# Quantizing in place, loading x earlier, and handing out averages and band runs one portion per score tile: a two-layer macaron kernel on one core

## The chip, the core and the metric

The kernel runs on one core of a Trainium2 chip. The metric is the device time of one execution in microseconds (us). A core has five engines that matter here: PE (TensorE, matmuls, with its weight loads shown apart as PEld), DVE (VectorE), ACT (ScalarE), POOL (GpSimd), and SP (SyncE), whose queue issues nearly all DMAs. Each engine works through its own instructions in order; semaphores join them.

## The reference, cut to what matters

Sixteen sequences of 512 tokens with 128 features pass through two layers. Layer 0, which the change touches, is a half-step feed-forward network, an attention, and the same feed-forward network again:

```
x = x + 0.5 * ffn(layernorm(x))      # both inputs of each matmul quantized to FP4 in blocks of 16
x = x + attn(layernorm(x))           # 16 heads of 8 features
x = x + 0.5 * ffn(layernorm(x))

# attn: relative positions clipped to +-64
dist  = clip(idx[None,:] - idx[:,None], -R, R) + R
score = einsum('bhqd,bhkd->bhqk', q, k) + einsum('bhqd,qkd->bhqk', q, rel_emb_k[dist])
attn  = softmax(score)
ctx   = einsum('bhqk,bhkd->bhqd', attn, v) + einsum('bhqk,qkd->bhqd', attn, rel_emb_v[dist])

# fp4 quantize and dequantize, blocks of 16
scale = max(max|xb| / 6, 1e-12);  q = GRID[searchsorted(MID, |xb/scale|)] * sign(xb) * scale
```

Layer 1 (mixture of experts with a small attention inside, linear attention, mixture of experts) follows; its code is the same in both kernels.

## The kernel before, in words

**Units.** Layer 0 works on halves of sequences. A unit `u = 2*b + half` holds the 256 query tokens of half `half` of sequence `b`; there are 32 units. For a unit, the scores of all 16 heads against 512 keys are cut into 4 key tiles `kt` of 128 keys and 8 blocks `bb` of 32 queries: 32 score tiles of 128 x 512, one PSUM bank each.

**Two passes over the scores.** `maxima` computes each score tile once (L263, and L267 for the relative positions where the tile is near the diagonal, "in the band") and reduces it on DVE with L341 (`mx`). At the end of a unit the maxima go through a small chain (`mk`, `mt`, `mn`) and two rounds of DMA (`MD`, then row 28 of `BD`), so that the second pass gets scores with the maximum already subtracted. `main` computes the tiles again and ACT takes the exponential into `PT` (L369), a buffer per key tile with three slots. Score tiles of both passes share a PSUM pool with three banks (`pS`, tiles `sps`). The maxima run about one and a half units ahead of the exponentials (47 tiles).

**Averages and band runs.** After the 8 score tiles of a key tile, `main` issues 16 matmuls `PT` times `V` that accumulate in `av0` and `av1` (L272, L274: "the averages"). Where all key tiles that reach a group of four query blocks are done, it issues the matmuls with the relative value embeddings into `rps` (same lines: a "band run" for two blocks at a time), and four ACT copies from `rps` to `RV` (L403: "band copies"). In half 0 the two groups are complete after `kt` 1 and 2, in half 1 both after `kt` 3. At the end of a unit, `RV` goes to DRAM (`RD`) and comes back reordered (`cr`), and ACT copies `av` to `cx` (L412). `av0`, `av1` and `rps` have one buffer each.

**Around it.** `fin` of a unit adds `cx` and `cr`, divides (L430 to L434), projects (L437 to L440) and adds into x. `head` and `tail` are the two feed-forward networks, each run on half a tile of x by `half`: layer norm (L55 to L62), the quantizer `quant_steps` (L65 to L82), matmuls (L121, L125), the quantizer again, matmuls (L139). `prep` and `prepV` make q, k and v for a later tile. The quantizer writes its scaled copy into a buffer `q_y` and its rounding constant into `q_M`.

**The order.** Each of these is a Python generator that yields between steps. `interleave` holds them all, each with a number of steps `n` and a stretch from `f` to `t` in units of `u`, and always advances the one whose next step is due first:

```
k=min(live,key=lambda r:r[3]+(r[4]-r[3])*r[2]/r[1])
```

`main` counts 59 steps in its unit: 32 score tiles, four empty steps after each key tile's averages, two after each band run of two blocks, one after the band copies, one at the end. The maxima of all units are one generator with 33 steps a unit. What is issued this way is then ordered on each engine by the framework's scheduler, which also hands out buffers; `run` keeps the matmuls of one burst together.

**x.** A tile of x (the 512 tokens of one sequence, 256 KB) lives in the pool `xk` with five buffers, from its load (`xload`, called in `head`, three of them before the loop) to the store of its tail to `X2` (L486). `head` of tile b+3 starts 0.1 units before unit 2b.

Of the kernel before, what the change touches and what calls it, by code (L numbers as in the profile page):

```python
# [8 lines left out]
F32 = mybir.dt.float32  # L9
# [16 lines left out]
class K:  # L26
# [37 lines left out]
    def quant_steps(s, X, wk, P, nb, tag):  # L64

        nc=s.nc
        n=nb*16
        X3=X.rearrange("p (b k) -> p b k",k=16)
        sc=wk.tile([128,nb],F32,name=tag+"_sc"); ri=wk.tile([128,nb],F32,name=tag+"_ri")
        nc.vector.tensor_reduce(sc[:P],X3,axis=AX.X,op=ALU.max,apply_absolute_value=True)  # L70
        nc.vector.tensor_scalar(sc[:P],sc[:P],float(np.float32(1/6)),1e-12,ALU.mult,ALU.max)
        nc.vector.reciprocal(ri[:P],sc[:P]); yield
        y=wk.tile([128,max(704,n)],F32,name=("q_y","q_yw")[n>704])[:,:n]; y3=y.rearrange("p (b k) -> p b k",k=16)
        nc.vector.tensor_tensor(y3[:P],X3,ri[:P].unsqueeze(2).to_broadcast([P,nb,16]),ALU.mult); yield
        M=wk.tile([128,max(704,n)],F32,name=("q_M","q_Mw")[n>704])[:,:n]
        nc.vector.tensor_scalar(M[:P].bitcast(U32),y[:P].bitcast(U32),0x7F800000,None,ALU.bitwise_and)
        nc.vector.tensor_scalar(M[:P],M[:P],1.0,C_MAG,ALU.max,ALU.mult); yield
        nc.vector.scalar_tensor_tensor(y[:P],y[:P],SHRINK,M[:P],ALU.mult,ALU.add); yield  # L78
        nc.gpsimd.tensor_tensor(M[:P],y[:P],M[:P],ALU.subtract)  # L79
        M3=M.rearrange("p (b k) -> p b k",k=16)  # L80
        nc.gpsimd.tensor_tensor(M3[:P],M3[:P],sc[:P].unsqueeze(2).to_broadcast([P,nb,16]),ALU.mult)
        yield M  # L82

class FFN:
# [22 lines left out]
    def half(f, xb, half, wk, pp):  # L107

        s=f.s; nc=s.nc
        xh=xb[:,2*half:2*half+2,:]  # L110
        xn=wk.tile([128,2,128],F32,name="f_x")
        yield from s.ln_steps(xh,xn,wk,2)
        for xq in s.quant_steps(xn.rearrange("p a b -> p (a b)"),wk,128,16,"xq"): yield
        ps=pp.tile([128,512],F32,name="mps")
        for j in range(2): nc.tensor.transpose(ps[:,j*128:(j+1)*128],xq[:,j*128:(j+1)*128],s.ident)
        xqT=wk.tile([128,256],F32,name="f_x"); nc.scalar.copy(xqT,ps[:,:256]); yield
        h=wk.tile([128,2,I],F32,name="f_h")
        for j in range(2):
            t=h[:,j,:]
# [26 lines left out]
class Attn0:  # L146
# [119 lines left out]
                w0=kt*128-blk*32-x+a.OFF  # L266
                nc.tensor.matmul(out[:,x*64:x*64+64],a.ET[:,w0:w0+128],TQ[:,:,b*32+4*x:b*32+4*x+4],start=False,stop=(x==7),skip_group_check=True)  # L267

    xnT={}; pend={}; last=None
    def run(a, mms):  # L270

        r=a.nc.tensor.matmul(*mms[0][0],**mms[0][1])  # L272
# [85 lines left out]
    def main(a, b, half, X, wk, big, pS, pA, pM):  # L358
        s=a.s; nc=a.nc; i=b%2
        u=(2*b+half)%3; BD=a.BD[u]; TQ=a.TQ[u]; KS=a.KS[b%2]; V=a.V[b%2]; RD=a.RD[half]; cr=a.cr[0]  # L360
        av=[pA.tile([128,512],F32,name=f"av{z}") for z in range(2)]
        RV=wk.tile([128,4,4,4,16],F32,name="RV")
        PT=[None]*4
        for kt in range(4):
            pt=big.tile([128,16,256],F32,name="PT"); PT[kt]=pt
            for bb in range(8):
                ps=pS.tile([128,512],F32,name="sps")
                a.scores(ps,kt,half,bb,BD,TQ,KS)
                nc.scalar.activation(pt[:,:,bb*32:bb*32+32].rearrange("p h (x j) -> p x h j",j=4),ps.rearrange("p (x h j) -> p x h j",x=8,j=4),AF.Exp)  # L369
                yield  # L370
            vs=a.vers(kt,half)
            mms=[]
            for z in range(4):
                for cg in range(4):
                    h=z*4+cg
                    o=av[z//2][cg*32:cg*32+32,(z%2)*256:(z%2)*256+256]
                    fs=(kt==0 and z%2==0)
                    mms.append(((o,V[:,2*kt-1+vs,h*9:h*9+32],pt[:,h,:]),dict(start=fs,stop=(kt==3),skip_group_check=True,tile_position=(0,cg*32))))
            a.run(mms)
            for _ in range(4): yield  # L380
            for hb in range(2):
                bl=range(hb*4,hb*4+4)
                ks=[k for k in range(4) if any(a.inband(k,half*8+x) for x in bl)]
                if max(ks)!=kt: continue
                rps=pA.tile([128,512],F32,name="rps")
                first=[True]*4
                mms=[]
                for b0 in bl[::2]:
                    ok=[(bb,k) for k in reversed(ks) for bb in (b0+1,b0) if a.inband(k,half*8+bb)]
                    for n,(bb,k) in enumerate(ok):  # L390
                        blk=half*8+bb
                        for x in range(8):
                            cg=x%4; col=(bb-hb*4)*128+(x//4)*64
                            v0=(blk*32-k*128+a.UO)//8
                            mms.append(((rps[cg*32:cg*32+32,col:col+64],a.TV[a.vers(k,half)][:,x,v0-8*a.vers(k,half):v0-8*a.vers(k,half)+4,:].rearrange("p v d -> p (v d)"),
                                PT[k][:,:,bb*32+4*x:bb*32+4*x+4]),
                                dict(start=first[cg],stop=(k==min(q for p,q in ok if p==bb)),skip_group_check=True,tile_position=(0,cg*32))))
                            first[cg]=False
                    a.run(mms); mms=[]
                    yield  # L400
                    yield
                for c in range(4):
                    nc.scalar.copy(RV[:,:,c,:,hb*8:hb*8+8].rearrange("p j z a -> p a z j"),rps.rearrange("p (a z c j) -> p c a z j",a=8,z=4,j=4)[:,c])  # L403
                yield

        nc.sync.dma_start(RD[:,:4*8*1024].rearrange("x (r f) -> x r f",f=1024),RV)
        for c in range(4):
            src=bass.AP(tensor=RD.tensor,offset=RD.offset+c*64,ap=[[1024,8],[8*1024+256,16],[1,64]])
            nc.sync.dma_start(cr[c*32:c*32+8].rearrange("p (xj f) -> p xj f",f=64),src)
        cx=wk.tile([128,4,256],F32,name="cx")  # L410
        for zz in range(2):
            nc.scalar.copy(cx[:,2*zz:2*zz+2,:].rearrange("p z (b j x) -> p (z b) x j",j=4,x=8),av[zz].rearrange("p (y x j) -> p y x j",x=8,j=4))  # L412
        a.pend[b,half]=cx,cr
        yield

    def fin(a, b, half, X, wk, pM):

# [28 lines left out]
def interleave(*gens):  # L446

    live=[[g,n,0,f,t] for g,n,f,t in (q if len(q)==4 else (*q,0,1) for q in gens)]
    while live:
        k=min(live,key=lambda r:r[3]+(r[4]-r[3])*r[2]/r[1])  # L450
        try: next(k[0]); k[2]+=1
        except StopIteration: live.remove(k)
# [4 lines left out]
def layer0(tc, s, w, src, dst, nb=16):  # L457
    nc=tc.nc
    tok=lambda x,b: x[b].rearrange("(t p) d -> p t d",p=128)
    P="L0_attn_"; names=["W_qkv","b_qkv","W_out","b_out","rel_emb_k","rel_emb_v"]  # L460
    with ExitStack() as c:
# [5 lines left out]
        pA=c.enter_context(tc.tile_pool(name="pA",bufs=1,space=PS))  # L467
        wk=c.enter_context(tc.tile_pool(name="wk",bufs=1))
        fk=c.enter_context(tc.tile_pool(name="fk",bufs=2))
        xk=c.enter_context(tc.tile_pool(name="xk",bufs=5))  # L470
        X={}
        def xload(b):
            if b in X or b>=nb: return
            t=xk.tile([128,4,128],F32,name="x"); X[b]=t
            nc.sync.dma_start(t,tok(src,b))
        def head(b,h):

            if b<nb: xload(b); yield from F.half(X[b],h,fk,pF)
        def prep(b):
            if b<nb: yield from A.prep(b,X[b],wk,pM)  # L480
        def prepV(b):
            if b<nb: yield from A.prepV(b,pM)
        def tail(b,h):
            if b<0: return
            yield from F.half(X[b],h,fk,pF)
            nc.sync.dma_start(tok(dst,b)[:,2*h:2*h+2,:],X[b][:,2*h:2*h+2,:])  # L486
# [15 lines left out]
                if next(st,0)==0: return  # L502
                yield
        pl,hl=2,3
        W=dict(part=0,V=(.6,.7),fin=(.45,.9),prep=(0,.7),tail=1.0,head=(-.1,1))
        with tc.tile_pool(name="wp",bufs=1) as wp:
            for b in range(3): xload(b)
            F=FFN(s,w["L0_ffn_w_gate"],w["L0_ffn_w_up"],w["L0_ffn_w_down"],wp,pF)
            ffn2=lambda f,b: interleave((f(b,0),21,0,.8),(f(b,1),21,.2,1))
            ffn2(head,0)  # L510
            A=Attn0(s,wp,pS,*[w[P+n] for n in names])
            def run(g):
                for _ in g: pass
            run(prep(0)); run(prepV(0)); loads(0); run(mxs(0,0))
            FFN1.pre(s,wp,[pA.tile([128,512],F32,name=f"av{z}") for z in range(2)]+[pA.tile([128,512],F32,name="rps")],w)
# [3 lines left out]
        for b in range(nb):  # L519
            for h in range(2):  # L520
                u=2*b+h
                def at(g,n,f,t): S.append((g,n,u+f,u+t))
                at(A.main(b,h,X,wk,big,pS,pA,pM),59,0,1)
                fn,tl=(W['fin'],W['tail']) if u<2*nb-2 else ((.3,.5),.6)
                at(A.fin(b,h,X,wk,pM),5,1+fn[0],1+fn[1])
                at(tail(b,h),21,1+fn[1]+.001,1+fn[1]+tl)
                if b+hl<nb: at(head(b+hl,h),21,*W['head'])
                if h==0 and b+pl<nb: at(prep(b+pl),11,*W['prep'])
                if h==1 and b+1<nb: at(prepV(b+1),1,*W['V'])
        interleave(*S)  # L530


# [505 lines left out]
```

## Time and profile before

| | |
|---|---|
| median of the runs | 3629.37 us (3628.54 to 3629.66) |
| the profiled execution | 3633.94 us |
| its span, first to last instruction | 3632.2 us |
| mean granted PE clock | 0.90 |
| busy: PE, DVE, ACT, POOL | 2825.0, 2444.9, 1693.8, 838.9 us |
| exponentials of layer 0 (L369) | 175.5 to 1974.5 us, 1024 of them, 0.60 us each |
| maxima of layer 0 (L341) | 126.4 to 1921.8 us, 1024 of them, 0.70 us each |

How to read it: the first half of the span, to about 2045 us, is layer 0, and 1800 us of that are the 32 units. Busy time of PE is modelled, since matmuls are pipelined. A wait is written as "engine, tile, line <- what ended it: total us, times, longest". In a line of the timeline, the first number is the start in us, the second the time taken, and a bracket at the end gives the idle time of the engine just before and what ended it. PEclk is the granted clock of PE as a share of full speed.

### The profile page before, as it was taken

The page shows a single profiled execution, that of the slowest core. Times are in us where ns is not written, and L with a number is a line of the kernel's source. Part 1 is how long each engine was busy: PE and PEld are TensorE (multiplying, and loading weights), DVE is VectorE, ACT ScalarE, POOL GpSimd, SP SyncE. Part 2 cuts the span into 40 slices and gives each one's busy share as a digit, 9 for nine tenths or more (in the row PEclk, how much of TensorE's full clock was granted, in tenths as well). Part 3 has the DMA queues.
Part 4 walks back from the last instruction along what each step waited for, and adds up shares of the span by engine and source line. Part 5 has one row for each costly group of instructions (what it writes and reads, how often), then busy time and mean ns, then how long its engine had stood idle before and what let it go on. Part 6 is the DMA issues. An engine that isn't in the chain of part 4 may idle for free. (4 is left out here: it accounts for less than half of the span.)

```text
span 3632.2 us, 95259 instructions
## 1 busy us (share of the span) xinstructions
PE 2825.0 (78%) x40077; PEld 2032.3 (56%) x40077; DVE 2444.9 (67%) x6508; ACT 1693.8 (47%) x3391; POOL 838.9 (23%) x789
## 2 busy tenths in 40 slices
PE   5578989889898889888896388873788888878570
PEld 3357777667676677666775244431565555555230
DVE  5568788777887788877773467774546655655356
ACT  3145555545455454545554155533455454445242
POOL 4122222222222222222110222212112211111226
PEclk8799999999999999999998599886899989989785
DMA  3232222321223222222210111104312222121401
GB/s 105 54 91 71 57 53 59 81 63 52 65 65 77 64 50 58 76 74 62 53 33 19 32 33 36 36 33 123 90 54 73 59 63 56 36 62 36 126 17 46
DMA packets 290159, 217.23 MB, mean 60 GB/s; under 512 B 77402, under 2 KB 257476, under 8 KB 289604
## 3 DMA queue, kind: packets, MB, share of 16 engines
q1 hardware_dynamic: 284468, 207.72, 21.6%
q8 instruction: 315, 5.16, 0.6%
q10 hardware_dynamic: 5264, 3.43, 0.4%
q14 instruction: 112, 0.92, 0.1%
HBM read 110.28 MB, written 100.78 MB: 58 GB/s over the span
## 5 line engine op out<-in xcount | busy, mean ns | idle before, releaser
L341 DVE TRANSPOSE_TENSOR_REDUCE mx<-sps 128x16 f32<-128x512 f32 x1024 | 702.5, 701 | 261.7 <-PE sps L263 137.2
L263 PE MATMUL sps<-a_BD,a_KS 128*128 128x128 f16 x8192 | 736.4, 222 | 136.2 <-DVE mx L341 65.6
L369 ACT ACTIVATE PT<-sps 128x512 f32<-128x512 f32 x1024 | 576.4, 599 | 433.8 <-PE sps L267 238.1
L263 PEld LDWEIGHTS <-a_KS 128*128 128x128 f16 x8192 | 546.1, 98 | 296.4 <-issue 260.0
L59 POOL TENSOR_TENSOR ln_rs<-ln_ve,negh 128x4 f32<-128x4 f32 (+1 forms) x192 | 176.9, 930 | 855.1 <-DVE ln_ve L58 760.6
L267 PE MATMUL sps<-a_TQ,a_ET 128*128 128x64 f16 x7168 | 370.3, 195 | 0.0
L721 DVE SCALAR_TENSOR_TENSOR moe<-mps,oh,moe 128x128 f32<-128x128 f32 x896 | 289.8, 341 | 110.7 <-PE mps L719 96.5
L79 POOL TENSOR_TENSOR q_M<-q_y,q_M 128x704 f32<-128x704 f32 (+2 forms) x129 | 157.0, 1218 | 784.6 <-DVE q_y L78 658.6
L719 PE MATMUL mps<-f_W,T 128*128 128x512 f32 x512 | 297.1, 701 | 24.8 <-DVE moe L721 20.0
L267 PEld LDWEIGHTS <-a_ET 128*128 128x128 f16 x7168 | 311.2, 99 | 2.3 <-issue 1.9
L274 PE MATMUL av<-PT,a_V 128*32 128x256 f32 x3840 | 251.9, 387 | 0.0
L894 DVE TENSOR_TENSOR a_at<-pp,a_cm 128x1024 f32<-128x1024 f32 x128 | 154.3, 1214 | 79.6 <-PE pp L892 78.6
L892 PE MATMUL pp<-a_F 64*128 64x128 f32 x2048 | 169.8, 306 | 41.4 <-DVE a_at L894 30.2
L892 PEld LDWEIGHTS pp<-a_F 64*128 64x128 f32 x2048 | 143.3, 206 | 93.0 <-DVE a_at L894 36.9
L719 PEld LDWEIGHTS mps<-f_W,T 128*128 128x128 f32 x512 | 102.7, 222 | 125.0 <-issue 75.3
L274 PEld LDWEIGHTS av<-PT,a_V 128*32 128x32 f32 x3840 | 121.4, 111 | 68.7 <-issue 5.0
L874 ACT ACTIVATE a_F<-pp 128x1024 f32<-128x1024 f32 x128 | 127.0, 1025 | 46.8 <-PE pp L872 40.5
L62 ACT ACTIVATE xn<-xn,ln_mr,ln_rs 128x128 f32<-128x128 f32 x256 | 103.6, 481 | 95.5 <-DVE ln_mr L60 75.2
L274 PE MATMUL rps<-PT,a_TV 128*32 128x64 f32 x6912 | 134.5, 222 | 4.6 <-issue 4.4
L139 PE MATMUL mps<-wdT,hT 128*128 128x128 f32 (+1 forms) x768 | 126.9, 301 | 5.6 <-ACT hT L136 4.0
L673 ACT COPY f_PT<-St 32x512 f32<-32x512 f32 x128 | 78.7, 615 | 106.0 <-DVE St L672 99.9
L872 PE MATMUL pp<-a_QK,a_PK 128*128 128x512 f16 x256 | 82.7, 413 | 54.4 <-DMA a_QK<-a1d 26.6
(342 smaller groups left out, 5330.2 us busy)
## 6 DMA issues: line engine op xcount, KB each, us to landing
QM<-a_HM SPq DMA_DIRECT2D x180, 128.0 KB
a_TQ<-QM SPq DMA_DIRECT2D x120, 192.0 KB
RD<-RV SPq DMA_DIRECT2D x32, 512.0 KB
a_KS<-KSd SPq DMA_DIRECT2D x128, 96.0 KB
a_QK<-a1d SPq DMA_DIRECT2D x128, 96.0 KB
xn<-X SPq DMA_DIRECT2D x32, 256.0 KB
a1d<-a_hi SPq DMA_DIRECT2D x64, 128.0 KB
a_BD<-QS SPq DMA_DIRECT2D x128, 58.0 KB
```

Source lines behind the costliest of these rows:

```text
L59: nc.gpsimd.tensor_tensor(rs,ve,s.negh[:,:n],ALU.pow); yield
L79: nc.gpsimd.tensor_tensor(M[:P],y[:P],M[:P],ALU.subtract)
L263: nc.tensor.matmul(o4[:,g],KS[:,sd,g*512+kt*128:g*512+(kt+1)*128],BD[:,g,:,b*32:b*32+32].rearrange("p h (x j) -> p x h j",j=4),start=(g==0 ...
L267: nc.tensor.matmul(out[:,x*64:x*64+64],a.ET[:,w0:w0+128],TQ[:,:,b*32+4*x:b*32+4*x+4],start=False,stop=(x==7),skip_group_check=True)
L274: for p,q in mms[1:]: a.nc.tensor.matmul(*p,**q)
L341: with a.s.tc.high_priority(): r=nc.vector.tensor_reduce(mx[:,kt,:,bb],ps.rearrange("p (i c) -> p i c",c=32),axis=AX.X,op=ALU.max,apply_tr ...
L369: nc.scalar.activation(pt[:,:,bb*32:bb*32+32].rearrange("p h (x j) -> p x h j",j=4),ps.rearrange("p (x h j) -> p x h j",x=8,j=4),AF.Exp)
L719: nc.tensor.matmul(ps,yT[:,j*128:(j+1)*128],a.W[:,e2*4:e2*4+4,:],start=True,stop=True)
L721: nc.vector.scalar_tensor_tensor(moe[:,j,:],ps[:,e*128:(e+1)*128],oh[:,j,e2*4+e:e2*4+e+1],moe[:,j,:],ALU.mult,ALU.add)
L874: nc.scalar.activation(f,ps,AF.Relu)
L892: nc.tensor.matmul(ps[:,hh,bs],f[hh*64:hh*64+64,1,bs],f[hh*64:hh*64+64,0,bs],start=True,stop=True)
L894: nc.vector.tensor_tensor(k,ps.rearrange("p h (b q) -> p (h b) q",b=4),a.cm.unsqueeze(1).to_broadcast([128,8,128]),ALU.mult)
```

## The change

Four things change in layer 0; no arithmetic and no instruction count does.

1. The quantizer works in place: the scaled copy is written over its input, and `q_y` goes. Tiles named `f_x` get three buffers instead of two.
2. `xk` has seven buffers. Four tiles are loaded before the loop, and tile b+4 is loaded by a generator of its own, due 0.35 units before unit 2b+1, instead of in its head (due 0.1 units before unit 2b+2).
3. Averages, band runs, band copies and the end of a unit become portions in a list `todo`. One portion is taken off after each score tile, so those of a key tile are issued with the score tiles of the next key tile, and those of the last one with the first key tile of the next unit. `main` counts 32 steps. After the last unit, `rest` issues what is left.
4. `fin` is due from 0.6 to 1.0 of the next unit instead of 0.45 to 0.9 (the last two units keep their own times); the tail after it moves with it.

```diff
 # quant_steps
-        y=wk.tile([128,max(704,n)],F32,name=("q_y","q_yw")[n>704])[:,:n]; y3=y.rearrange("p (b k) -> p b k",k=16)
+        y=X; y3=X3
 # FFN.half
-        xn=wk.tile([128,2,128],F32,name="f_x")
+        xn=wk.tile([128,2,128],F32,name="f_x",bufs=3)
...
-        xqT=wk.tile([128,256],F32,name="f_x"); nc.scalar.copy(xqT,ps[:,:256]); yield
+        xqT=wk.tile([128,256],F32,name="f_x",bufs=3); nc.scalar.copy(xqT,ps[:,:256]); yield
 # Attn0
-    xnT={}; pend={}; last=None
+    xnT={}; pend={}; last=None; todo=[]
 # Attn0.main
+        def avrun(kt):
+            if kt==0: T["av"]=[pA.tile([128,512],F32,name=f"av{z}") for z in range(2)]
...
+            a.run(mms)
+        def rvrun(hb, b0, ks):
+            if b0%4==0: T["rps"]=pA.tile([128,512],F32,name="rps"); T["first"]=[True]*4
...
+            a.run(mms)
+        def rvcopy(hb):
+            if hb==0: T["RV"]=wk.tile([128,4,4,4,16],F32,name="RV")
+            for c in range(4):
+                nc.scalar.copy(T["RV"][:,:,c,:,hb*8:hb*8+8].rearrange("p j z a -> p a z j"),T["rps"].rearrange("p (a z c j) -> p c a z j",a=8,z=4,j=4)[:,c])
+        def end():
+            nc.sync.dma_start(RD[:,:4*8*1024].rearrange("x (r f) -> x r f",f=1024),T["RV"])
...
+            a.pend[b,half]=cx,cr
         for kt in range(4):
             pt=big.tile([128,16,256],F32,name="PT"); PT[kt]=pt
             for bb in range(8):
                 ps=pS.tile([128,512],F32,name="sps")
                 a.scores(ps,kt,half,bb,BD,TQ,KS)
                 nc.scalar.activation(pt[:,:,bb*32:bb*32+32]...,AF.Exp)
+                if a.todo: a.todo.pop(0)()
                 yield
-            vs=a.vers(kt,half)
...
-            a.run(mms)
-            for _ in range(4): yield
+            a.todo.append(lambda kt=kt: avrun(kt))
             for hb in range(2):
                 bl=range(hb*4,hb*4+4)
                 ks=[k for k in range(4) if any(a.inband(k,half*8+x) for x in bl)]
                 if max(ks)!=kt: continue
-                rps=pA.tile([128,512],F32,name="rps")
...
-                    a.run(mms); mms=[]
-                    yield
-                    yield
-                for c in range(4):
-                    nc.scalar.copy(RV[...])
-                yield
+                a.todo+=[lambda hb=hb,b0=b0,ks=ks: rvrun(hb,b0,ks) for b0 in bl[::2]]+[lambda hb=hb: rvcopy(hb)]
+            if kt==3: a.todo.append(end)
+    def rest(a):
+        while a.todo: a.todo.pop(0)(); yield
 # layer0
-        xk=c.enter_context(tc.tile_pool(name="xk",bufs=5))
+        xk=c.enter_context(tc.tile_pool(name="xk",bufs=7))
...
-            if b<nb: xload(b); yield from F.half(X[b],h,fk,pF)
+            if b<nb: yield from F.half(X[b],h,fk,pF)
+        def xl(b):
+            xload(b); yield
...
-        W=dict(part=0,V=(.6,.7),fin=(.45,.9),prep=(0,.7),tail=1.0,head=(-.1,1))
+        W=dict(part=0,V=(.6,.7),fin=(.6,1.0),prep=(0,.7),tail=1.0,head=(-.1,1))
...
-            for b in range(3): xload(b)
+            for b in range(4): xload(b)
...
-                at(A.main(b,h,X,wk,big,pS,pA,pM),59,0,1)
+                at(A.main(b,h,X,wk,big,pS,pA,pM),32,0,1)
...
+                if h==1 and b+hl+1<nb: at(xl(b+hl+1),1,-.35,-.3)
...
+        S.append((A.rest(),8,2*nb,2*nb+.15))
         interleave(*S)
```

## The prediction

> **What bounds the kernel now.** I began with the slices of the page, which show no engine full, then took the steady stretch of layer 0 alone, 422 to 1692 us. The first exponentials (L369) of units 4 and 26 start there, so it is 22 units of 57.7 us. The columns are busy time with the instruction count behind it, then clock, DMA share and GB/s.
>
> ```profile
> core 0: us, PE busy (x) PEld busy (x) DVE busy (x) ACT busy (x) POOL busy (x), PEclk, DMA share, GB/s
> 422.00:1692.00 1270.00, 1126.22 (x20068) 889.03 (x20065) 1013.48 (x2274) 647.68 (x1430) 306.91 (x287) 0.98 0.25 64
> ```
>
> Per unit that is 51.2 us of PE, 46.1 of DVE, 29.4 of ACT. PE comes nearest to a bound, but 6.5 us of each unit it stands idle, and the time goes to engines that wait for each other. Who waits for whom in the same stretch (total us, times, longest):
>
> ```profile
> PE sps L263 <- DVE mx L341: 40.1, 45, 3.9
> PE sps L263 <- ACT PT L369: 21.6, 56, 0.8
> PE mps L437 <- DVE a_V L321: 19.2, 11, 1.8
> PE mps L440 <- ACT cn L438: 11.4, 9, 1.8
> DVE ln_st L55 <- DMA x<-in_L_attn_x_dram: 41.1, 10, 5.2
> SPq L475 <- DMA X<-x: 26.0, 10, 3.4
> ```
>
> The first and fifth rows belong together. The head of a new tile of x issues its load when it is due (L475); the fifth buffer is then still being stored, so the load waits on SP, and DVE, which works in order, stands 4.1 us (41.1/10) before the first statistic. Meanwhile the maxima (L341) queued behind it leave the three score buffers full, and PE stops. In time, on DVE and PE:
>
> ```profile
> 879.93 1.07 DVE L55 BATCH_NORM_STATS2 ln_st<-x 128x6 f32<-128x128 f32 x5 [4.11 <-DMA x<-in_L_attn_x_dram]
> 882.54 0.39 PE L263 MATMUL sps<-a_BD,a_KS 128*128 128x128 f16 x4 [2.85 <-DVE mx L341]
> 884.61 0.58 PE L263 MATMUL sps<-a_BD,a_KS 128*128 128x128 f16 x4 [0.42 <-DVE mx L341]
> 884.99 0.63 PE L267 MATMUL sps<-a_TQ,a_ET 128*128 128x64 f16 x8
> 888.38 0.39 PE L263 MATMUL sps<-a_BD,a_KS 128*128 128x128 f16 x4
> ```
>
> The third and fourth rows show a second price: after the stop the same groups take 0.58 and 0.63 us, where they take 0.39 and 0.40 elsewhere, until 888 us.
>
> **The order, before and after.** In the built programs PE's order in units 4 to 25 can be counted. Before, score tiles for the exponentials come 275 times in pairs, 11 times in threes and 121 times alone, and those for the maxima come up to nine in a row. Changed, both kinds alternate: 660 single ones of each and 22 pairs of each. All three engines keep their instructions; layer 1 moves by a few places. A tile costs PE 0.24 us out of the band and 0.47 in it (starts of such groups at 873.18, 873.66 and 873.89 us), ACT 0.60 (L369) and DVE 0.70 (L341).
>
> **The change, part by part.**
>
> *a. x loaded ahead.* The load of tile b+4 stands 1.25 units (72 us) before its head, with seven buffers and no store left to wait for. Thirteen tiles (3 to 15) are loaded inside the loop: 13 x 2.85 us of PE stop = 37 us. Bounds: 0, if DVE's lost time is then lost elsewhere, and 13 x 4.14 = 54. I take 37, since PE is the engine nearest to its bound. What is late next: the same head's scale (L59 on POOL), with a DVE that has work meanwhile.
>
> *b. The slow spells after stops.* A mean clock of 0.98 in the row above is about 0.02 x 1270 = 25 us of lost full clock in 22 units. Bounds 0 and 25; I take 15, as the stops of (a) and (d) that start most of these spells shrink.
>
> The Trainium skill, "TensorE: Matmul & The Clock Gate", section "HAM oscillation — how this bites in real kernels", speaks against (b): its rule is to avoid idle gaps of PE over about 3.4 us, so a stop of 2.85 us should cost nothing more. The rows at 884.61 and 884.99 show that here it did. By the rule (b) is 0 and the forecast 3577 us.
>
> *c. Pairs of exponentials.* PE waits for L369 because two or three such tiles come in a row while ACT needs 0.60 each. With a maxima tile between them this wait has no cause left: 22 us, from the second row. Bounds 0 and 31 (21.6 stretched from 22 units to 32).
>
> *d. The output projection (L437, L440).* Before, L440 stands two tiles behind the transposes whose copy it needs, and PE waits; L437 waits for a DVE that does prepV's V first. With `fin` moved from (.45,.9) to (.6,1) it leaves prepV's place (.6,.7) on DVE, and in the built order four to six tiles and the averages stand between L437 and L440. 19.2 + 11.4 = 31 us at most, 0 at least; I take 20. The last two units keep (.3,.5), so the end of the layer stays.
>
> *e. What the portions add.* The averages of a key tile now stand on PE behind one maxima tile and the first score tile of the next key tile, on average; before, mostly behind two maxima tiles. They need the last exponential, 0.60 us and about 0.1 of hand-over. The two tiles cover 0.47 to 0.94 us. Queued behind a waiting average is everything on PE, and through the three score buffers DVE and ACT. Covered it is 0; never covered 128 x 0.7 = 90 us. The near row is small (L272 waits for L369 in all 7.4 us), so I take 0.1 each, 13 us. In odd units the first band run stands right behind a score tile whose exponential it needs: 16 x 0.7 = 11 us, bounds 0 and 11. The fourth load at the start is 256 KB more at the 146 GB/s of the first 60 us: up to 2 us, and 1 more for reordered starts. Sum +27, bounds 0 and +104.
>
> *f. At nothing.* In place, the quantizer issues the same operations on other buffers. `f_x` and `f_h` are held until POOL's subtraction (L79, 1.67 us at 704 wide); a third `f_x` and the half unit until the next `f_h` cover that. Without cover, one such POOL operation for each of the 64 halves is 107 us at most. Band copies (L403, four of 0.42 us) and `cx` copies (1.08 us) only move to the next key tile; RD's DMAs follow them by up to a quarter unit, 14 us, while `fin` moves 0.15 units, 9 us. On SP these DMAs stand behind the x load and ahead of the QS and QM stores of the tile two ahead, which have over a unit of slack. One X2 store stands among the loads of BD and TQ; if its tail is late, the loads are, with some 28 us until their first score.
>
> Sum: -37 - 15 - 22 - 20 + 27 = -67 us. The profiled execution took 3633.9 (span 3632.2 and 1.7 around it) and the median of the runs is 3629.4, 4.6 lower. So 3567 for a profile like this one and **3562 us** for the median. A unit would fall from 57.7 to about 55.3 us. With all bounds it is 3488 to 3733.
>
> **Rivals.** *Slower: the averages wait.* ACT now has its fixed work in the first key tile of even units, two `cx` copies (2.16 us) and four band copies (1.68) between exponentials. If the last exponential runs late by one such copy, each average stops PE, and everything behind it, by about 1 us: +128 +14 against -94, some 3677 us. It decides from (94-14)/128 = 0.6 us for each average. Against it: ACT is busy 51% of the stretch, and the small row above.
>
> *Hidden anyway.* DVE's 4.1 us may be work that it catches up, as it idles 20% of the time; then only (c) or (d) pays and (e) takes it back: -22 +27 -4 of (d), close to no change, 3630.
>
> *The order matters more than its stops.* If alternation also ends the starving of ACT (L369 waits 154.4 + 113.9 us for PE in the stretch) and the unit falls to PE's present 51.2 us plus 1.5, 32 units gain 5 us each: 3470 us.
>
> *Not what it says.* If the scheduler had put the portions back together there would be no alternation; the built order excludes that.
>
> **How the numbers follow.** Forecast, with its own range 3508 to 3622: 0.62. Slower: 0.19. Hidden: 0.09. More than forecast: 0.10. The range of 3508 to 3650 leaves out most of the last and the upper half of the slower case, under 0.2. About 0.2% (7 us) is what a measurement of this kernel can tell from no change. Faster takes the first, the fourth and a little of the hidden case, 0.74; same 0.07; slower 0.19.
>
> **What would show it.** Right: no L55 wait for x, PE's wait for L341 near 10 us in 22 units, for L369 under 5, clock 0.99, units near 55 us. Wrong: rows "PE av L272 <- ACT PT" of tens of us, L263 still waiting for L341 with DVE full of other work, or L263 waiting for DMA of BD or TQ.

## The result and the profile after

The changed kernel takes 3863.01 us (median of four runs, 3856.82 to 3876.84) against 3629.51 for the kernel before: a ratio of 1.0636, interval 1.0602 to 1.067. It is slower, where the forecast was faster, and lies beyond every bound that the prediction worked out. The profiled execution took 3858.58 us. From its page, the first line and the row of granted clock in 40 slices:

```profile
span 3856.9 us, 95214 instructions
PEclk8788888898889889888999859897699889999775
```

The same row of the kernel before:

```profile
PEclk8799999999999999999998599886899989989785
```

The first half of the clock row, which is layer 0, stands mostly at 8 where the kernel before had 9. The time is lost there: the 32 units run from 181.8 to 2211.6 us, 2029.7 us against 1799.6 before. That is +230.1, and the whole profiled execution grew by 224.6. The same steady stretch as in the prediction, units 4 to 25, in the same columns:

```profile
439.00:1895.00 1456.00, 1168.62 (x20068) 953.69 (x20069) 1056.72 (x2259) 661.30 (x1428) 317.27 (x283) 0.88 0.22 56
```

The 22 units take 186 us more with the same 20068 matmuls: 42 us are PE busy for longer at a clock of 0.88 instead of 0.98 (1168.6 against 1126.2), and 144 us are PE standing still (287.4 against 143.8). The loss is not even. An even unit, in which `prep` runs, takes 74.7 us on average where it took 57.2; an odd one takes 57.7 where it took 58.2. Who waits for whom in this stretch (total us, times, longest):

```profile
DVE qkhi L307 <- DMA QS<-qkhi: 93.9, 11, 9.5
DVE qklo L307 <- DMA KSd<-qklo: 82.6, 11, 7.9
PE sps L263 <- DVE mx L341: 129.7, 31, 8.2
PE sps L349 <- DVE mk L347: 75.7, 22, 4.6
PE mps L434 <- DVE cx L426: 45.6, 22, 3.3
PE sps L263 <- ACT PT L407: 21.3, 61, 0.7
PE rps L272 <- ACT PT L407: 7.7, 11, 0.8
```

The first two rows matter most: DVE, a compute engine, waits for DMAs that *store* what `prep` made. It can't need their data; it needs their buffer. `prep` of an even unit casts q into a buffer of tag `qkhi` and its rest into `qklo` (L143, L144), does the same for k, and stores them to `QS` and `KSd` (L302). Then L307 takes a small product of q apart in the same way, into buffers of the *same tags*. There are two of `qkhi` and one of `qklo`, so L307 has to wait until prep's own stores have landed: (93.9 + 82.6) / 11 = 16.0 us in each even unit. Before, the same line waited for DMAs 5.2 us in all, in the stretch 422 to 1692 us:

```profile
DVE qklo L307 <- DMA KSd<-qklo: 5.2, 5, 1.3
```

L341 is queued behind it on DVE, and PE waits for L341 (third row, 40.1 before). The row for the averages, on which the prediction's slower rival was built, is the last: 0.7 us, 11 times.

Unit 12 in time, on SP's queue, then on DVE, POOL and PE (start, time taken, in brackets the idle time just before and what ended it):

```profile
983.51 0.77 SPq L394 DMA_DIRECT2D RD<-RV  x1
994.44 1.37 SPq L397 DMA_DIRECT2D a_cr<-RD  x4
995.91 1.22 SPq L302 DMA_DIRECT2D QS<-qkhi  x2
997.23 7.65 SPq L300 DMA_DIRECT2D QM<-a_HM  x12
1004.92 1.42 SPq L302 DMA_DIRECT2D QS<-qklo  x1
1009.43 0.52 SPq L302 DMA_DIRECT2D KSd<-qklo  x1
```
```profile
980.50 0.38 DVE L143 CAST qkhi<-qk 128x512 f16<-128x512 f32 x1
999.05 0.68 DVE L307 CAST qkhi<-mps 32x512 f16<-32x512 f32 x1 [9.52 <-DMA QS<-qkhi]
1000.41 0.58 PE L263 MATMUL sps<-a_BD,a_KS 128*128 128x128 f16 x4 [8.19 <-DVE mx L341]
1008.24 1.16 POOL L144 TENSOR_TENSOR qklo<-xn,qkhi 128x512 f16<-128x512 f32 x1 [24.28 <-DMA QS<-qklo]
1011.77 0.68 DVE L307 TENSOR_TENSOR qklo<-mps,qkhi 32x512 f16<-32x512 f32 x1 [7.16 <-DMA KSd<-qklo]
```

q is cast at 980.50, but its store is issued only at 995.91. SP issues in order, and ahead of the store stands the read of `cr` (L397), which waits until `RD` has landed, 10.9 us after its issue. Then twelve `QM` stores stand ahead of `QS<-qklo`. POOL can't write the second `qklo` until that one has landed (24.28 us), so `KSd<-qklo` is late too, and DVE stops a second time. PE follows with stops of 8.19 us (third row) and, after the second one, 4.16; it restarts with 0.58 us for a group that takes 0.39 in the prediction's rows. The same queue and the same steps in unit 12 of the kernel before:

```profile
894.37 0.72 SPq L406 DMA_DIRECT2D RD<-RV  x1
904.28 1.37 SPq L409 DMA_DIRECT2D a_cr<-RD  x4
907.44 0.43 DVE L143 CAST qkhi<-qk 128x512 f16<-128x512 f32 x1 [1.42 <-ACT qk L291]
907.89 1.69 SPq L302 DMA_DIRECT2D QS<-qkhi  x2
921.16 0.52 SPq L302 DMA_DIRECT2D KSd<-qklo  x1
923.72 0.68 DVE L307 TENSOR_TENSOR qklo<-mps,qkhi 32x512 f16<-32x512 f32 x1 [0.70 <-DMA KSd<-qklo]
```

The wait of `cr` for `RD` is nearly as long here (9.9 us), but it is over before q is cast, and the store goes out at once. Two things moved against each other. In the median of the even units 4 to 24, counted from the unit's first exponential, `RD` went from 8.0 to 15.7 us: the portions put the end of a unit further into the next one. The cast of q went from 21.0 to 12.8 us: prep's steps now stand some eight score tiles earlier. The two moves come from different parts of the change, as the traces of the experiments below show by the same count. Parts 1 and 2 alone (e1) put the cast at 9.8 us and leave `RD` at 9.3; part 3 alone (e5) leaves the cast at 19.0 us and puts `RD` at 11.4. The cast used to come 3.3 us after the issue of `cr` and now comes 13.1 us ahead of it. How long q's store then waits (from the cast to the first `QS<-qkhi`) went from 0.4 to 14.6 us.

### The profile page after: what moved, and what is told of

The parts are those of the page before. It is cut to its first block, busy times and chain, and to the rows that moved or that the text cites. A ratio compares the mean times of both kernels' runs of the same rounds, so it can differ in the third digit from the quotient of the medians.

```text
span 3856.9 us, 95214 instructions
## 1 busy us (share of the span) xinstructions
PE 2872.7 (74%) x40077; PEld 2108.4 (55%) x40077; DVE 2495.8 (65%) x6508; ACT 1714.4 (44%) x3391; POOL 852.9 (22%) x789
## 5 line engine op out<-in xcount | busy, mean ns | idle before, releaser
L407 ACT ACTIVATE PT<-sps 128x512 f32<-128x512 f32 x1024 | 605.5, 601 | 891.9 <-PE sps L267 474.4
L263 PE MATMUL sps<-a_BD,a_KS 128*128 128x128 f16 x8192 | 776.7, 232 | 234.3 <-DVE mx L341 168.4
L341 DVE TRANSPOSE_TENSOR_REDUCE mx<-sps 128x16 f32<-128x512 f32 x1024 | 709.1, 704 | 262.5 <-PE sps L267 140.7
L263 PEld LDWEIGHTS <-a_KS 128*128 128x128 f16 x8192 | 591.7, 104 | 390.0 <-issue 355.8
L267 PE MATMUL sps<-a_TQ,a_ET 128*128 128x64 f16 x7168 | 391.0, 200 | 0.1
L267 PEld LDWEIGHTS <-a_ET 128*128 128x128 f16 x7168 | 332.3, 103 | 1.4 <-DMA a_TQ<-QM 0.4
L726 PE MATMUL mps<-f_W,T 128*128 128x512 f32 x512 | 291.7, 689 | 21.3 <-DVE moe L728 16.9
L79 POOL TENSOR_TENSOR q_M<-f_h,q_M 128x704 f32<-128x704 f32 x64 | 113.9, 1780 | 647.0 <-DVE f_h L78 560.1
L426 DVE TENSOR_TENSOR cx<-cx,a_cr 128x512 f32<-128x512 f32 x64 | 114.3, 1842 | 39.9 <-DMA a_cr<-RD 39.9
```

The source lines that it names most:

```text
L263: nc.tensor.matmul(o4[:,g],KS[:,sd,g*512+kt*128:g*512+(kt+1)*128],BD[:,g,:,b*32:b*32+32].rearrange("p h (x j) -> p x h j",j=4),start=(g==0 ...
L341: with a.s.tc.high_priority(): r=nc.vector.tensor_reduce(mx[:,kt,:,bb],ps.rearrange("p (i c) -> p i c",c=32),axis=AX.X,op=ALU.max,apply_tr ...
L426: nc.vector.tensor_tensor(o,o,cr.rearrange("p (x j z b s) -> p s (z b) x j",x=4,j=4,z=4,s=2)[:,s2],ALU.add)
L726: nc.tensor.matmul(ps,yT[:,j*128:(j+1)*128],a.W[:,e2*4:e2*4+4,:],start=True,stop=True)
```

## The experiments

The theory: the loss is L307's wait for buffers. Rivals: the later `fin`, the portions as such (averages and ACT copies between the exponentials), prep's earlier place. Ratios are to the kernel before, run beside each kernel on the same chip; unit times are means over even and odd units from 4 to 25. Waits of an experiment are from the stretch 422 to 1692 us where nothing else is said.

**Part by part.** Three kernels with only some of the change. In the third, both halves of the head load the tile, so x is read a second time over what the first half had computed; its time holds these loads and the waits for them, and e5 below replaces it.

```diff
 # e1: parts 1 and 2 only (in place, seven buffers, loads ahead)
         W=dict(...,fin=(.45,.9),...)          # as before; main as before, 59 steps
 # e2: e1 and part 4
+        W=dict(...,fin=(.6,1.0),...)
 # e3: part 3 alone; quantizer, loads of x and fin as before
```

> Only parts 1 and 2 of the change: quantization in place and x loaded ahead; main, its 59 steps and fin at (.45,.9) as before. Theory S (store queue): the loss comes from the portions, which put the band output's round trip through DRAM later on SP, ahead of prep's stores of q and k, while prep itself stands earlier; without portions it is absent, and the x wait is gone: even and odd units near 56 us, 3570 to 3600 us, no wait of L307 over 2 us. Rival Q (in place): buffers held until POOL's subtraction stall the quantizers; then this kernel is slow already, over 3750 us.

> As e1, with fin moved to (.6,1.0). Theory S: as e1 within 20 us, since the band output's round trip stays at the end of the unit. Rival F (fin later): the addition of cx and cr, 1.1 us before and 2.1 us in the changed kernel, collides with the tail's quantizer, and this kernel is slower than e1 by 50 us or more.

> Only part 3: portions and 32 steps, with the quantizer's own buffer, five tiles of x, loads in head and fin at (.45,.9) as before. Theory S: nearly all of the loss is here, 3780 to 3900 us, with L307 waiting for DMA by 8 us or more in even units and even units over 70 us. Rivals Q and F: the portions alone do no harm, 3560 to 3640 us.

| | us | ratio | interval | even / odd unit |
|---|---|---|---|---|
| e1, loads ahead and in place | 3608.35 | 0.9929 | 0.9902 to 0.9956 | 61.9 / 52.6 |
| e2, and fin later | 3761.38 | 1.0343 | 1.0318 to 1.0368 | 70.4 / 54.6 |
| e3, portions (x loaded twice) | 3816.7 | 1.049 | 1.0464 to 1.0516 | 62 / 67 |

No single part carries the loss. The loads gain, but less than they should: the odd units get 5.6 us shorter and the even ones longer. e2, without any portions, already loses 3.4%. The wait is in both, as `KSd<-qklo` before L307: 51.1 us in e1 and 83.8 in e2. So the theory as it was put for these two, that without portions the wait is absent, was too narrow; the buffers stay as the cause to test. In e3 DVE waits 117.4 us for loads of x (20 times), which says nothing of the change.

**The wait taken away.** The results of L307 get buffers of their own, 1 KB a partition each; to make room, x has six buffers instead of seven. prep's steps keep the place that they have in the changed kernel's built order.

```diff
-        rhi=wk.tile([128,512],F16,name="qkhi",bufs=2)[:32]; rlo=wk.tile([128,512],F16,name="qklo")[:32]
+        rhi=wk.tile([128,512],F16,name="rhi")[:32]; rlo=wk.tile([128,512],F16,name="rlo")[:32]
-        xk=c.enter_context(tc.tile_pool(name="xk",bufs=7))
+        xk=c.enter_context(tc.tile_pool(name="xk",bufs=6))
```

> The changed kernel with buffers of their own for the two results of L307 (rhi, rlo), so that L307 never waits for the stores of q and k; six tiles of x instead of seven to make room. Theory S: L307's waits (16 us in each even unit) are the loss; they vanish, even units fall from 75 to about 60 us and the time to 3600 to 3660 us. Rival P (portions as such, or L426 and the chain behind the maxima): it stays over 3780 us.

Measured: 3609.24 us, 0.9932 (0.9907 to 0.9958). With everything else as in the changed kernel, 7.0 points of the ratio are gone (6.6 to 7.5, from the two intervals). An even unit takes 58.6 us, 16.1 less than in the changed kernel, where L307's wait was 16.0. The stretch of units 4 to 25, and PE's waits for the maxima in it:

```profile
404.00:1655.00 1251.00, 1117.00 (x20082) 905.96 (x20083) 1040.00 (x2261) 660.26 (x1429) 298.29 (x284) 0.95 0.25 65
```
```profile
PE sps L263 <- DVE mx L341: 3.8, 16, 0.3
```

The wait of 129.7 us is 3.8, and the clock is back from 0.88 to 0.95. This settles what made the change slower.

**Portions alone, done cleanly.** As e3, with each tile of x loaded once.

```diff
         def xload(b):
+            if b in X or b>=nb: return
```

> Only part 3 (portions, 32 steps), everything else as before; it replaces e3, whose edit also loaded each tile of x a second time. Theory S (prep's results wait for prep's own stores, which stand late on SP): L307 still waits for DMA, 4 to 8 us in each even unit, and the time is 3660 to 3800 us. Rival P (alternation costs by itself): slower than before with no large L307 wait.

Measured: 3689.53 us, 1.0126 (1.0111 to 1.0141), even and odd units 66.1 and 52.8. Both waits are there, the old one for x and the new one:

```profile
DVE qklo L307 <- DMA QS<-qkhi: 50.4, 11, 5.1
DVE ln_st L55 <- DMA x<-in_L_attn_x_dram: 31.2, 11, 3.7
```

**Is it SP's queue?** Two kernels leave the buffers shared and take either the stores or what they stand behind off SP: e6 issues the `QS` and `KSd` stores of L302 on ACT, e12 issues `RD` and the reads of `cr` on POOL.

```diff
 # e6
-                nc.sync.dma_start((QS,KSd)[z][:,p*8:p*8+8,:],t)
+                nc.scalar.dma_start((QS,KSd)[z][:,p*8:p*8+8,:],t)
 # e12
-            nc.sync.dma_start(RD[...],T["RV"])
+            nc.gpsimd.dma_start(RD[...],T["RV"])
-                nc.sync.dma_start(cr[...],src)
+                nc.gpsimd.dma_start(cr[...],src)
```

> The changed kernel with the stores of q, k and their remainders (L302) issued from ACT's queue instead of SP's. Theory S: on SP they stand behind RD's round trip of 10 us and behind 12 QM stores of 7.6 us; off SP they go as soon as they are made, L307's wait falls from 16 us in each even unit to under 4, and the time to 3600 to 3700 us. Rival D (the stores are slow in landing wherever they are issued): L307 waits as before, over 3800 us.

> The changed kernel with RD's write and the four reads of cr issued from POOL's queue, so that SP does not stand in front of prep's stores for RD's 10 us. Theory S in its narrow form (RD's round trip in front of the stores is what makes them late): L307's first wait, 8.5 us in each even unit, shrinks to under 3; the time falls by 60 to 200 us, less what POOL's own standing costs the quantizers. Rival E (prep merely comes too early for its two buffers): the first wait stays over 6 us.

e6: 3803.44 us, 1.0439 (1.0418 to 1.046). e12: 3836.87 us, 1.0549 (1.0521 to 1.0577). They win back 2.0 and 0.9 of the 7.0 points, since the place of the wait changes. Waits in e6, then in e12:

```profile
DVE qkhi L143 <- ACT xn L293: 103.1, 10, 11.0
PE sps L263 <- ACT PT L407: 70.3, 58, 6.1
```
```profile
POOL a_cr L397 <- DMA RD<-RV: 203.7, 20, 12.2
DVE qklo L307 <- DMA KSd<-qklo: 79.5, 10, 8.9
```

In e6 L307 no longer waits for these stores, but ACT now stands, and DVE waits for ACT's part of prep and PE for its exponentials. Both times fell less than was expected. In e12 the first of L307's waits is nearly gone (4.9 us in the stretch), so SP's order was its cause. The second stays. POOL now stands while `RD` lands, so the first `qklo` and the copy that four of the `QM` stores need come late, and the second `qklo` has to wait for `QS<-qklo`, which stands behind all twelve. In unit 12 they held SP's queue for 11.73 us, where it was 7.65 in the changed kernel:

```profile
974.49 11.73 SPq L300 DMA_DIRECT2D QM<-a_HM  x12
988.76 1.15 POOL L144 TENSOR_TENSOR qklo<-xn,qkhi 128x512 f16<-128x512 f32 x1 [7.83 <-DMA QS<-qklo]
```

The DMA that waits for `RD` makes its engine's queue stand on POOL as it did on SP: 203.7 us here, 200.6 us (22 times) on SP in units 4 to 25 of the changed kernel.

**prep later.** In the changed kernel, `prep` is due from 0.3 to 1.0 of the unit instead of 0 to 0.7.

```diff
-        W=dict(part=0,V=(.6,.7),fin=(.6,1.0),prep=(0,.7),...)
+        W=dict(part=0,V=(.6,.7),fin=(.6,1.0),prep=(.3,1),...)
```

> The changed kernel with prep due from .3 to 1.0 of its unit instead of 0 to .7, so that its stores come after RD's round trip on SP and L307 does not come before them. Theory S: L307 waits less than 4 us in each even unit, 3600 to 3680 us. Rival D (the wait belongs to the two shared buffers wherever prep stands): over 3780 us.

Measured: 3728.25 us, 1.025 (1.0215 to 1.0285). The cast of q now comes 47.5 us into the unit, long after `cr`, its store goes out 0.7 us later, and L307 waits 5.9 us in the whole stretch. The order of cast and `cr` is thus enough to make the wait or to end it. The time, though, misses the range that was expected: even and odd units take 60.5 and 61.2 us, and PE's wait for the exponentials (L263 for L407) has grown from 21.3 to 72.5 us. Most of that is a wait of the same kind on another engine. `RV` has one buffer, and ACT's band copies (L391) wait until `RD` has emptied it:

```profile
ACT RV L391 <- DMA RD<-RV: 47.2, 11, 5.1
```

The next exponential is queued behind them, and PE waits for that. In unit 12:

```profile
939.19 1.02 ACT L391 COPY RV<-rps 128x128 f32<-128x128 f32 x4 [4.67 <-DMA RD<-RV]
940.69 0.59 PE L263 MATMUL sps<-a_BD,a_KS 128*128 128x128 f16 x4 [4.50 <-ACT PT L407]
```

Eleven such stops of PE, each over 2 us, make 45.6 of the 72.5 us. No run here gave `RV` a second buffer.

**What the parts are worth without the wait.** Three more kernels with L307's own buffers (and six tiles of x): e8 is e1, e7 is e2, e10 is the changed kernel with the old times of `fin`. e9 is that last one without own buffers.

```diff
 # e9, e10 (portions); e8 (no portions)
-        W=dict(...,fin=(.6,1.0),...)
+        W=dict(...,fin=(.45,.9),...)
```

> e2 (in place, loads ahead, fin at (.6,1), no portions) with buffers of their own for L307's results and six tiles of x. Theory S: e2's loss of 153 us against e1 was the same wait of L307, so it is gone: 3580 to 3640 us. Against e4 (3609 us, the same with portions) it tells what the portions do once the wait is away: alternation by my forecast is worth 20 to 50 us, so this kernel would be at 3630 to 3660. Rival F (fin later costs by itself): over 3700 us.

> e1 (in place, loads ahead, fin at (.45,.9), no portions) with buffers of their own for L307's results. Theory S: e1 still lost 51 us to L307 in 22 units (4.6 us each in eleven of them), so 3540 to 3585 us, the fastest so far. Rival H (such waits are caught up elsewhere): within 10 us of e1, 3600 to 3615.

> The changed kernel with fin back at (.45,.9); portions, loads ahead and shared buffers stay. Theory S: moving fin alone cost 153 us without portions (e2 against e1), most of it by L307's wait, since prep then stands earlier in the built order; so here 60 to 150 us come back, 3710 to 3800 us, and L307's waits fall from 16 us in each even unit to 6 to 10. Rival P (the portions alone place RD late, and fin has no part): 3830 to 3870 us.

> The changed kernel with buffers of their own for L307's results and fin back at (.45,.9): the last corner beside e4 (portions, fin late), e7 (no portions, fin late) and e8 (no portions, fin early). If the portions are worth the 28 us that e4 gains on e7 wherever fin stands: 3535 to 3560 us, faster than e8. If fin's place is what they mended: equal to e8 or slower, 3570 to 3620 us.

All with the loads ahead and in place; each cell gives the ratio, then the even unit:

| | shared buffers | own buffers | less in an even unit | L307's wait with shared |
|---|---|---|---|---|
| fin early, no portions | e1 0.9929, 61.9 | e8 0.9808, 57.5 | 4.4 | 4.6 |
| fin late, no portions | e2 1.0343, 70.4 | e7 1.0009, 62.1 | 8.3 | 8.4 |
| fin early, portions | e9 1.0115, 66.8 | e10 0.9902, 61.3 | 5.5 | 8.0 |
| fin late, portions | changed 1.0636, 74.7 | e4 0.9932, 58.6 | 16.1 | 16.0 |

(Intervals: e7 0.9994 to 1.0025, e8 0.9793 to 0.9822, e9 1.0084 to 1.0145, e10 0.9872 to 0.9933.) In three of four rows the wait is worth what it takes, to 0.2 us; in the third the even unit gains 2.5 us less than that, and where they went is not shown. The wait grows with both the later `fin` and the portions, which is why no part carries it alone. Where neither is there, with own buffers, the kernel is the fastest of all: **e8, 3572.68 us, 0.9808**, faster than both kernels of the case. Its units 4 to 25, and PE's wait for the maxima in them:

```profile
417.00:1631.00 1214.00, 1114.07 (x20078) 875.45 (x20075) 1015.77 (x2264) 652.67 (x1430) 295.88 (x285) 0.99 0.27 67
```
```profile
PE sps L263 <- DVE mx L341: 34.6, 103, 1.3
```

55.2 us a unit and a clock of 0.99. PE still waits for the maxima, but in 103 pieces of a third of a microsecond, and no longer in stops of 2.85 us.

Without the wait, the later `fin` costs 2.0 points without portions (e7 against e8, some 76 us) and 0.3 with them (e4 against e10, within the intervals). The portions cost 0.9 points with the early `fin` (e10 against e8) and gain 0.8 with the late one. Added to e8, each of them loses. In e7 PE waits where it did not in e8:

```profile
PE sps L263 <- DVE mx L341: 50.2, 54, 1.8
PE sps L349 <- DVE hq_sc L71: 25.3, 11, 2.3
```

So the later `fin` goes with more work on DVE in the way of the maxima. An even and an odd unit together take 6.7 us longer in e7 (117.0 against 110.3). PE's wait at L349 was 4.4 us in e8, so the two rows are (50.2 - 34.6 + 25.3 - 4.4) / 11 = 3.3 of it. Where the rest goes stays open, and so does why prep's steps stand earlier once parts 1 and 2 are in.

## Why the prediction was wrong

**The step that failed is (f), "At nothing".** It saw that RD's DMAs would move, by up to 14 us (7.7 measured), and asked who is late because of it: "On SP these DMAs stand behind the x load and ahead of the QS and QM stores of the tile two ahead, which have over a unit of slack." The slack was counted to the *reader* of `QS`, which comes a unit later. A store has a second customer: the next writer of the buffer that it empties. Here that is L307, a few steps later in the same prep, on DVE, the engine whose stops leave the three score buffers full. It had no slack at all: in the kernel before, L307 already waited 0.70 us in unit 12. The step had no upper bound for this, so "with all bounds" ended at 3733. Own buffers took off 7.0 points, or about 256 us at 3637 us a run; without this term the changed kernel gains 0.7%. The same step's other worry, that quantizing in place could make POOL hold the quantizers up, did not come true: e1 and e8 quantize in place and are faster than the kernel before.

The same step was blind on the other side. "All three engines keep their instructions" was right, but which steps of `prep` stand at which score tile was not counted; the cast of q moved 8.2 us earlier, about as much as RD moved later, and by e1 it was the loads or the quantizing in place that moved it.

**(a) x ahead: right.** No wait of L55 for x is left, and in e8 the maxima stop PE for 1.3 us at the longest. Together with (b) it was put at 52 us; e8, which is this part with L307's wait taken off, gains 1.9%, some 70 us.

**(b) the slow spells: right in kind.** The clock was 0.99 in e8, and 0.88 where the stops got longer instead of shorter. The term's sign turned with the stops. That the clock rose from 0.98 to 0.99 when these stops went agrees with the prediction's rows. Against the rule that the prediction quotes they say little: the longest of the stops before took 3.9 us, over the rule's bound, so only the spells behind the shorter ones, as at 884.61, speak against it, and no run here took such a stop alone.

**(c) alternation: worth nothing.** PE's wait for the exponentials "has no cause left", it said, 22 us. It is 21.3 us in the changed kernel, and 28.5 in e4, where nothing else hides it. ACT's other work is not the reason: in 58 of the 61 times ACT had itself been idle, waiting for PE, just before that exponential. The two wait for each other in turn, as in unit 13 of the changed kernel:

```profile
1062.88 0.61 PE L263 MATMUL sps<-a_BD,a_KS 128*128 128x128 f16 x8 [0.32 <-ACT PT L407]
1063.30 0.60 ACT L407 ACTIVATE PT<-sps 128x512 f32<-128x512 f32 x1 [0.47 <-PE sps L263]
```

What keeps the other score buffers from helping there was not followed.

**(d) fin later: wrong sign.** The two waits it named (L437 for V, L440 for the copy) are gone from the list, as forecast. But -20 us became +76 (e7 against e8), or nothing with portions; the price of what `fin` meets in its new place was not in the sum.

**(e) the portions' own waits: right.** 11 waits of 0.7 us in the 11 odd units, as worked out; the averages stay covered. The slower rival, which made them wait, had the right sign for a wrong reason. "Hidden anyway" and "the order matters more" fell as well.

## What to carry to other kernels

When a transfer moves later, ask two questions of everything queued behind it: who reads the data, and who writes next into the buffer that the transfer empties. A row in which a compute engine waits for a *store* points at a buffer that is missing; here even 5 us of it in the profile before marked a step without slack, and two buffers of 1 KB a partition turned a loss of 6.4% into a gain of 0.7%. Count the built order not only for the steps that a change edits but for the others that share their queues, since a merge by due time moves those too.

## What the runs showed of the hardware

An addition on DVE of two operands in SBUF can take twice as long beside POOL. The group that adds `cr` to `cx`, over the whole span of the changed kernel (count, busy us, mean ns, idle time before it):

```profile
L426 DVE TENSOR_TENSOR cx<-cx,a_cr 128x512 f32<-128x512 f32 x64 | 114.3, 1842 | 39.9 <-DMA a_cr<-RD 39.9
```
The mean before was 1119 ns. In the changed kernel 50 of the 64 overlap an elementwise operation of POOL and take 1.43 to 2.33 us, 2.18 in the median; the 14 that don't take 1.10. Before, one of 64 overlapped. Not every overlap costs: in e9, 14 of the 26 additions that overlap keep 1.09 to 1.11 us. PE waits for this sum at L434, 45.6 us in the stretch. In unit 12, two of them beside the quantizer's steps on POOL:

```profile
1019.17 2.20 POOL L79 TENSOR_TENSOR q_M<-f_h,q_M 128x704 f32<-128x704 f32 x1 [9.77 <-DVE f_h L78]
1020.78 3.79 DVE L426 TENSOR_TENSOR cx<-cx,a_cr 128x512 f32<-128x512 f32 x2
1021.45 2.15 POOL L81 TENSOR_TENSOR q_M<-q_M,hq_sc 128x704 f32<-128x704 f32 x1
```

POOL's subtraction (L79) takes 2.20 us here where the prediction has 1.67, so both sides pay. The Trainium skill, "SBUF — State Buffer", section "🔬 SBUF: two separate sides", says that a DVE operation with two SBUF inputs and a GpSimd operation that reads SBUF contend for a port pair which one of them holds for its whole instruction. These rows agree that the two meet. They do not show one that holds and one that waits: L79 started 1.61 us ahead of the first addition, and yet both are longer.
